# A quantised gated layer on one core: the order of the first three weight slots, and one weight turned by a transfer

## The chip, the core and the metric

The kernel runs on one core of a Trainium2 chip. The core has five engines, each with its own queue, worked off in order: TensorE (PE) multiplies matrices out of the on-chip memory SBUF into the accumulators (PSUM, eight banks of 128 x 512 fp32); VectorE (DVE), ScalarE (ACT) and GpSimd (POOL) work element by element; SyncE (SP) issues most transfers (DMA) between main memory and SBUF, or inside SBUF. Engines wait for each other by semaphores, which the framework derives from the tiles that each instruction reads and writes. The metric is the device time of one execution in microseconds (us). Of the kernel before, three executions took 729.2, 729.31 and 729.77: a median of 729.31.

## The reference

`x` is 4 x 1024 x 512 (4 sequences, b = 0 to 3), `cond` is 4 x 128, `up_w` 4096 x 512, `down_w` 512 x 2048, all fp32.

```python
scale = cond @ norm_w.T + 1.0
h = x * (scale[:, None, :] * rsqrt(mean(x * x, -1) + 1e-6))
u = h @ up_w.T
val, gate = split(u, 2, axis=-1)
h = val * gelu(gate)                       # 2048 columns
hq = round(h * 127 / max|h| per row), undone again
wq = weights of down_w as -1, 0, 1 times their mean size
out = hq @ wq.T + x
```

## The kernel before

**Tiles and batches.** A batch is one sequence, 1024 tokens, held as two halves (h = 0, 1) of 512. The 2048 columns of `val` and of `gate` are cut into 16 slots of 128 (j = 0 to 15); weight tile Wj holds the 128 `val` rows and the 128 `gate` rows of slot j (t = 0 and t = 1). fp32 operands are split into a high and a low fp16 part, and a product is high x high + high x low + low x high. The outputs of slot j are kept in SBUF in tile `H`, piece j; the pieces of `H` not yet in use (8 to 17, and 4 to 7 at the start) hold weights, tokens and scratch.

**Batch 0** multiplies plainly: `plain_half(j, h)` does 12 matmuls for the gate (`pg`), then Gelu on ScalarE, then 12 for the value (`pv`), then one VectorE instruction that joins the two. Between the two products it can call a function, `between`. `plain_first` is the same for slot 0, half 0, with its 24 matmuls in another order, and it calls `second_part` after 6 and `second_slot` after 16 of them.

**Batches 1 to 3** use a fast matrix product with seven products for eight (`slot`, `product`, lines 594 to 604 and 668 to 721). It needs sums and differences of quarters of each Wj. Those are made during batch 0: `s_sums` (POOL, into scratch `sf`), `s_high` (ScalarE), `s_low` (POOL) make seven fp16 planes, and `s_spill` writes them to main memory. `s_load_x` and `s_load_y` bring them back, for each slot of each later batch, on SP's queue.

**How a weight gets ready.** `w_load` brings the fp32 rows, `w_range` finds a power of two for each row (VectorE), `w_scale` scales them (POOL for j < `ROWS`, else ScalarE), and then the tile has to be turned, columns to rows:

- for j < `ROWS` (0, 1, 2): `w_turn` with TensorE transposes into two banks `pw`, `w_high` (ScalarE) and `w_low` (VectorE) out of them, and `w_evac` copies both banks to `wf(j)` in fp32, from which `s_sums` reads the turned quarters;
- for j >= `ROWS` (3 to 15): `w_rows` splits the rows into high (ScalarE) and low (VectorE), and one transposing transfer on SP (line 359) turns them. `s_sums` reads the unturned rows, the spilled sums are rows, and `s_load` turns them when it loads (its `turn`, line 427).

**How the tokens of batch 0 get ready.** `first_load` brings 2 x 128 tokens, `first_sum(n)` sums squares (ScalarE or VectorE), `rsqrt` makes the factors (for token groups 4 to 7: one VectorE instruction, then a power on POOL), `first_scale(n)` scales, `first_turn(n)` turns with four TensorE transposes, `first_high` and `first_low` write the fp16 parts. Groups 0 to 3 are half 0, groups 4 to 7 half 1; `other_half` turns half 1.

**Order.** The schedule is written out by hand: each engine runs its instructions in the order of the program text, and nothing is reordered. Before slot 3 the halves run in the order (0,0), (1,0), (2,0), (0,1), (1,1), (2,1); from slot 3 on `first_batch(j)` does both halves of a slot. In the later batches a small planner (`Filler`, lines 1246 to 1269) puts VectorE and ScalarE work for the previous batch into the slots by cost and due time; it is not touched. `cond_scale_rest`, `cond_largest` (VectorE), `cond_over` (a transpose on TensorE, `pm`), `cond_range` (VectorE) and `cond_spread` (TensorE, `pd`) prepare the scale of batches 1 to 3.

Lines that the prediction names: 343 transposes of weights, 358 and 359 the row split and its transfer, 367 to 379 `w_high` and `w_low`, 383 `w_evac`, 403 and 407 the sums, 615 and 658 the plain products, 935 and 937 `first_sum`, 964 `first_scale`, 985 warm-up matmuls, 289 and 286 weight loads, 924 token loads.

Of the kernel before, what the change touches and what calls it, by code (L numbers as in the profile page):

```python
# [39 lines left out]
Y_FROM, Y_TO = 3, 5  # L40
# [11 lines left out]
def glu_quant_kernel(  # L52
# [17 lines left out]
    NK = D // P  # L70
    NJ = FF // P
# [102 lines left out]
    def cond_load_rest():  # L174
        v = cond[1:].rearrange("b c -> (b c)").partition_broadcast(P)
        ACT.dma_start(out=cb[:, 1:].rearrange("p b c -> p (b c)"), in_=v)
# [90 lines left out]
    sg0 = sm.tile([P, NJ, 2], F32, name="sg_0", tag="sg")  # L267
    up_v = up_w.rearrange("(t j p) d -> j p t d", t=2, p=P)
    W_SLOT = {1: 12, 2: 13, 0: 14}
    W_EARLY = {6: 9, 7: 10, 8: 11}  # L270
    ROW_SLOT = {3: 8, 4: 15, 5: 16}
    iv = {}
    pw = {}

    def wn(j):
        return H[:, W_EARLY.get(j, W_SLOT[j % 3])]

    def wf(j):

        return H[:, 11 if j == 2 else 15 + j % 2].rearrange("p t (n f) -> p (t n) f", n=2)  # L280

    sf = H[:, 17].rearrange("p t (n f) -> p (t n) f", n=2)

    def w_load(j, ts=(1, 0)):
        if j > 2:
            SP.dma_start(out=wn(j), in_=up_v[j])
            return
        for t in ts:
            SP.dma_start(out=wn(j)[:, t], in_=up_v[j][:, t])
# [27 lines left out]
    def w_range(j, t0=0, t1=2):  # L317
        w_factor(j, w_largest(j, t0, t1), t0, t1)

    def w_gain(j):  # L320
        DVE.tensor_tensor(sg0[:, j, :], sw[:, j, :], dx[:, 0:1].to_broadcast([P, 2]), ALU.mult)

    ROWS = 3
    LATE = 6

    def w_scale(j, ts=(1, 0), eng=None):
        eng = eng or (ACT if j >= ROWS else POOL)
        for t in ts:  # L330
            w, r = wn(j)[:, t], iv[j][:, t : t + 1]
            if eng is ACT:
                ACT.activation(w, w, AF.Copy, scale=r)
            else:
                eng.tensor_scalar(w, w, r, 1.0, ALU.mult, ALU.mult)

    def w_turn(j, banks=None, ts=(1, 0)):
        if j not in pw:
            pw[j] = banks or [po_bank(f"pw_{j}_{t}") for t in (1, 0)]
        for t in ts:  # L340
            n = 1 - t
            for k in range(NK):
                PE.transpose(
                    pw[j][n][:, k * P : (k + 1) * P], wn(j)[:, t, k * P : (k + 1) * P], ident
                )
# [17 lines left out]
    def w_high(j, ts=(1, 0)):  # L363
        gate, a21, a22 = a_parts(j)
        g, v = (p.rearrange("p (n f) -> p n f", n=2) for p in pw[j])
        if 1 in ts:
            ACT.copy(gate[:, :, 0], g)
        if 0 in ts:
            ACT.copy(a21[:, 0], v[:, 0])
            ACT.copy(a22[:, 0], v[:, 1])  # L370

    def w_low(j, ts=(1, 0)):
        gate, a21, a22 = a_parts(j)
        g, v = (p.rearrange("p (n f) -> p n f", n=2) for p in pw[j])
        if 1 in ts:
            DVE.tensor_tensor(gate[:, :, 1], g, gate[:, :, 0], ALU.subtract)
        if 0 in ts:
            DVE.tensor_tensor(a21[:, 1], v[:, 0], a21[:, 0], ALU.subtract)
            DVE.tensor_tensor(a22[:, 1], v[:, 1], a22[:, 0], ALU.subtract)

    def w_evac(j):
        for n in range(2):
            ACT.copy(wf(j)[:, 2 * n : 2 * n + 2].rearrange("p n f -> p (n f)"), pw[j][n])

    def s_sums(j):
        if j >= ROWS:
            v = wn(j).rearrange("p t (n f) -> p t n f", n=2)
            a11, a12, a21, a22 = v[:, 1, 0], v[:, 1, 1], v[:, 0, 0], v[:, 0, 1]
        else:
            a11, a12, a21, a22 = (wf(j)[:, n] for n in range(4))  # L390
        POOL.tensor_tensor(sf[:, 0], a21, a22, ALU.add)
        POOL.tensor_tensor(sf[:, 2], a11, a21, ALU.subtract)
        POOL.tensor_tensor(sf[:, 1], sf[:, 0], a11, ALU.subtract)
        POOL.tensor_tensor(sf[:, 3], a12, sf[:, 1], ALU.subtract)
# [29 lines left out]
    def s_load(g, c0, c1, turn=False):  # L424
        s, d = s_tile(g)[:, c0:c1], s_dram[g % NJ, :, c0 * 2 * HALF : c1 * 2 * HALF]
        if turn:
            SP.dma_start_transpose(s.rearrange("p c w (k f) -> p (c w k) f", k=2), d)
        else:
            SP.dma_start(out=s.rearrange("p c w f -> p (c w f)"), in_=d)

    def s_load_x(g):
        s_load(g, Y_TO, C_ALL)
        s_load(g, 0, Y_FROM, g % NJ >= ROWS)

    def s_load_y(g):
        if g % NJ < ROWS:
            s_load(g, Y_FROM, Y_TO)
        else:
            s_load(g, Y_FROM + 1, Y_TO)
            s_load(g, Y_FROM, Y_FROM + 1, True)  # L440


    wmean = cpool.tile([P, 1], F32, name="wmean")
# [59 lines left out]
    def rsqrt(ssq, rs, eng=POOL):  # L503
        eng.tensor_scalar(ssq, ssq, 1.0 / D, EPS, ALU.mult, ALU.add)  # L504
        POOL.tensor_tensor(rs, ssq, neghalf[:, : rs.shape[-1]], ALU.pow)
# [129 lines left out]
    def plain_half(j, h, between=nothing):  # L635
        pg = bank(*(("A", 2) if h or j == 1 else ("B", 1)), name=f"pg_{j}_{h}")
        plain(j, 1, h, pg)
        t1 = wpool.tile([P, TOK], F32, name=f"g_{j}_{h}", tag="t1")
        ACT.activation(t1, pg, AF.Gelu, scale=gain(j, 1))
        between()  # L640
        pv = bank("E", 2, name=f"pv_{j}_{h}")
        plain(j, 0, h, pv)
        DVE.scalar_tensor_tensor(h_half(j, h), pv, gain(j, 0), t1, ALU.mult, ALU.mult)
# [279 lines left out]
    def first_load(n, m=1):  # L923
        SP.dma_start(
            out=X0[:, n : n + m],
            in_=xf[n * P : (n + m) * P, :].rearrange("(s p) d -> p s d", p=P),
        )
# [4 lines left out]
    def first_sum(n, eng=ACT):  # L932
        v, j, a = X0[:, n], junk[:, n % 4], ssq0[:, n : n + 1]
        if eng is ACT:
            ACT.activation(j, v, AF.Square, accum_out=a)
        else:
            eng.scalar_tensor_tensor(j, v, 1.0, v, ALU.mult, ALU.mult, accum_out=a)
# [21 lines left out]
    def first_scale(n, eng):  # L959
        r = rs0[:, n : n + 1]  # L960
        if eng is ACT:
            ACT.activation(X0[:, n], X0[:, n], AF.Copy, scale=r)
        else:
            eng.tensor_scalar(X0[:, n], X0[:, n], r, 1.0, ALU.mult, ALU.mult)
# [6 lines left out]
    def first_high(h, k, pt):  # L971
        c = slice(h * TOK, (h + 1) * TOK)
        ACT.activation(XP[:, 0, k, c], pt, AF.Copy, scale=scT[:, k, 0:1])

    def first_low(h, k, pt, eng=DVE):
        c = slice(h * TOK, (h + 1) * TOK)
        eng.scalar_tensor_tensor(  # L977
            XP[:, 1, k, c], pt, scT[:, k, 0:1], XP[:, 0, k, c], ALU.mult, ALU.subtract
        )

    def keep_warm(n):

        pz = bank("A", 2, name="pz")
        for i in range(n):
            PE.matmul(pz, warm[:, :P], warm, start=True, stop=True)
# [1 line left out]
    first_load(0, 2)  # L987
    first_load(2, 2)
    w_load(0)
    w_load(1)  # L990
    first_load(4, 2)
    first_load(6, 2)
    w_load(2)
    keep_warm(3)
    pc = cond_first_row()
# [4 lines left out]
    first_sum(0)  # L1000
    first_sum(1, DVE)
    root = rsqrt_root(0, 2)
    keep_warm(2)
    steps = cond_range_steps(pm, 0, 1)
    dg = next(steps)
    next(steps)
# [21 lines left out]
    w_range(0, 0, 1)  # L1028
    first_high(0, 0, ptx[0])
    w_high(0, (1,))  # L1030
    w_low(0, (1,))
    w_scale(0, (0,))
    w_gain(0)
    first_high(0, 1, ptx[1])
    first_high(0, 2, ptx[2])
    first_high(0, 3, ptx[3])
    cond_load_rest()
    w_range(1)
    w_gain(1)
# [3 lines left out]
    def second_part():  # L1043
        w_turn(0, ts=(0,))
        w_high(0, (0,))
        w_low(0, (0,))
        w_scale(1, (1,), ACT)
        for k in range(1, NK):
            first_low(0, k, ptx[k])
        ACT.activation(start_t, neghalf[:, 0:1], AF.Gelu)  # L1050


# [92 lines left out]
    def second_slot():  # L1145
        w_turn(1)
        w_high(1)
        w_low(1, (1,))
        w_range(2)
        w_gain(2)  # L1150
        w_scale(2)
        w_low(1, (0,))

    def third_slot():
        w_turn(2)
        w_high(2)
        w_low(2)
        w_evac(2)
        first_scale(4, ACT)
        first_scale(5, DVE)  # L1160
        first_scale(6, ACT)
        first_scale(7, DVE)

    def other_half():
        ptx = [po_bank(f"ptx_1_{k}") for k in range(3)] + [bank("A", 2, name="ptx_1_3")]
# [7 lines left out]
    w_load(3)  # L1173
    for n in range(4, ND):
        d_load(n)
    w_evac(0)
    w_evac(1)
    first_sum(4)
    first_sum(5)
    first_sum(6, DVE)  # L1180
    first_sum(7, DVE)
    rsqrt(ssq0[:, 4:8], rs0[:, 4:8], DVE)
    plain_half(1, 0, third_slot)
    w_load(4)
    s_sums(0)
    w_range(3)
    w_gain(3)
    plain_half(2, 0, other_half)
    w_load(5)
    for n in (2, 3):  # L1190
        d_load(n)
    w_scale(3)
    s_all(0)
    s_sums(1)
    cond_scale_rest()
    mx = cond_largest(1, B)
    plain_half(0, 1)
    w_range(4)
    w_gain(4)
    w_scale(4)  # L1200
    w_rows(3)
    s_all(1)
    s_sums(2)
    for n in D_SUM[0]:
        d_sum(n)
    pm = cond_over(mx, 1, B, "po")
    plain_half(1, 1)
    w_load(6)
    for n in (0, 1):
        d_load(n)  # L1210
# [402 lines left out]
```

## Time and profile before

The profile shows one execution; times in it are us from its first instruction.

| | us |
|---|---|
| median of three executions | 729.31 |
| the profiled execution | 728.31 |
| its span, first to last instruction | 726.5 |
| TensorE busy | 718.9 |
| VectorE busy | 582.6 |
| ScalarE busy | 398.0 |
| POOL busy | 193.4 |
| batch 0, slots 0 to 2 (TensorE's first product to slot 3) | 12.62 to 49.19 |
| batch 0, slots 3 to 15 | 49.19 to 184.69 |

A group line reads: source line, engine, operation, output <- input, shapes, count, busy us, mean ns of one, idle time before it and what ended it. In a timeline a line is: start, length, engine, line, operation, output <- input, count, and in brackets the idle time of that engine before it and its releaser. Names are those of tiles: `SXY` and part of `R` hold the turned weights, `H` weights, tokens and outputs, `pw`, `pg`, `pv`, `ptx`, `pm`, `pd`, `pz` are banks. The granted clock of TensorE is 1.00 in every slice.

### The profile page before, as it was taken

What the parts mean: (1) busy time and instruction counts of PE and PEld (TensorE: products, weight loads), DVE (VectorE), ACT (ScalarE), POOL (GpSimd) and SP (SyncE); (2) the same over time, 40 slices, a digit from 0 to 9 for tenths busy, and PEclk for the clock granted to TensorE, in tenths of its full rate; (3) what the DMA queues carried; (4) which work ended last, traced back from release to release, by engine and by line L of the source; (5) the groups of instructions that cost most, each with busy time, mean ns of one, the idle gap of its engine ahead of it and who ended that gap; (6) DMA issues with size and microseconds to landing.
All of it is one profiled execution on the core that took longest, in us unless ns stands there. A gap on an engine that the chain in (4) does not pass through costs nothing.

```text
span 726.5 us, 10149 instructions
## 1 busy us (share of the span) xinstructions
PE 718.9 (99%) x3662; PEld 359.0 (49%) x3662; DVE 582.6 (80%) x828; ACT 398.0 (55%) x627; POOL 193.4 (27%) x206
## 2 busy tenths in 40 slices
PE   8999999999999999999999999999999999999998
PEld 4544444444444446655444445665444444445844
DVE  8877888986698899788689897677678888755897
ACT  6869876772337674544335676544433665332374
POOL 1479887775100034340000030360020000000100
PEclk9999999999999999999999999999999999999999
DMA  7669999988344565867735646765934555442253
GB/s 266 223 189 298 284 291 231 252 202 231 116 102 102 131 145 139 208 161 166 179 98 103 131 102 176 201 151 163 223 102 100 84 121 103 101 102 89 97 180 115
DMA packets 203982, 117.30 MB, mean 161 GB/s; under 512 B 165382, under 2 KB 174487, under 8 KB 203932
## 3 DMA queue, kind: packets, MB, share of 16 engines
q1 hardware_dynamic: 203642, 116.33, 63.0%
q8 instruction: 28, 0.46, 0.3%
q10 hardware_dynamic: 290, 0.33, 0.2%
q14 instruction: 22, 0.18, 0.1%
HBM read 54.22 MB, written 23.09 MB: 106 GB/s over the span
## 4 chain that ended last, share of the span: by engine, by line
PE 92%; DVE 5%; DMA 1%; ACT 1%; issue 0%; SPq 0%; DVEq 0%; ACTq 0%
PE A L600 32%; PE E L600 16%; PE pg L615 11%; PE pv L615 10%; PE B L600 8%; PE po L868 8%; PE po_end L820 4%; PE po L820 1%; DVE gm L734 1%; DVE R L736 1%; DMA H<-in_x_dram 1%; DMA SXY<-H 1%; PE ptx L969 0%; PE pv L658 0%; DVE R L977 0%
## 5 line engine op out<-in xcount | busy, mean ns | idle before, releaser
L600 PEld LDWEIGHTS <-SXY 128*128 128x128 f16 x2016 | 197.2, 98 | 232.3 <-issue 0.7
L600 PE MATMUL A<-R,SXY 128*128 128x512 f16 x1152 | 266.3, 379 | 0.0
L600 PE MATMUL E<-R,SXY 128*128 128x512 f16 x576 | 140.0, 379 | 0.1
L698 DVE SCALAR_TENSOR_TENSOR H<-A,sg,t 128x512 f32<-128x512 f32 x48 | 36.0, 750 | 68.2 <-PE A L600 68.1
L792 DVE TENSOR_TENSOR H<-H,am 128x1024 f32<-128x1024 f32 x64 | 76.3, 1218 | 0.0
L615 PEld LDWEIGHTS <-SXY 128*128 128x128 f16 x486 | 47.4, 98 | 57.5 <-DMA SXY<-H 0.8
L750 POOL PARTITION_ALL_REDUCE am<-R x8 | 14.3, 1793 | 230.9 <-DVE R L736 230.9
L711 ACT ACTIVATE t<-t,sg 128x512 f32<-128x512 f32 x48 | 34.6, 721 | 69.3 <-DVE t L708 69.2
L600 PE MATMUL B<-R,SXY 128*128 128x512 f16 x288 | 70.0, 379 | 0.0
L734 DVE TENSOR_REDUCE gm<-H 128x512 f32<-128x1024 f32 x56 | 69.1, 1233 | 1.0
L615 PE MATMUL pg<-R,SXY 128*128 128x512 f16 x252 | 57.8, 379 | 0.3 <-DMA SXY<-H 0.3
L615 PE MATMUL pv<-R,SXY 128*128 128x512 f16 x234 | 54.4, 379 | 0.0
L695 ACT ACTIVATE t<-B,sg 128x512 f32<-128x512 f32 x48 | 33.0, 687 | 36.2 <-PE B L600 36.2
L678 ACT COPY t<-A 128x512 f32<-128x512 f32 x48 | 27.9, 582 | 39.8 <-PE A L600 39.5
L504 POOL TENSOR_SCALAR ssq<-ssq 128x2 f32<-128x2 f32 x12 | 3.9, 321 | 172.2 <-ACT xt L534 122.8
L868 PE MATMUL po<-wd,R 128*128 128x256 fp8e4 x384 | 48.5, 273 | 0.0
L800 ACT ACTIVATE H<-H 128x1024 f32<-128x1024 f32 x38 | 39.9, 1051 | 14.3 <-DVE H L792 14.3
L690 ACT COPY v<-E 128x512 f32<-128x512 f32 x48 | 28.1, 585 | 30.8 <-PE E L600 27.5
L868 PEld LDWEIGHTS <-R 128*128 128x128 bf16 (+1 forms) x416 | 40.7, 98 | 8.5
L717 DVE SCALAR_TENSOR_TENSOR H<-v,sg,t 128x512 f32<-128x512 f32 x48 | 38.0, 792 | 7.9 <-ACT t L711 7.9
L736 DVE TENSOR_TENSOR R<-R,gm 128x512 f32<-128x512 f32 x56 | 42.0, 750 | 1.3
L714 DVE TENSOR_TENSOR v<-A,v 128x512 f32<-128x512 f32 x48 | 32.9, 685 | 12.2 <-PE A L600 11.0
(207 smaller groups left out, 981.2 us busy)
## 6 DMA issues: line engine op xcount, KB each, us to landing
SXY<-s_dram SPq DMA_DIRECT2D x57, 256.0 KB, 3.1
s_dram<-SXY SPq DMA_DIRECT2D x18, 384.0 KB, 3.2
H<-in_L_cond_up_w_dram SPq DMA_DIRECT2D x13, 512.0 KB, 5.4
SXY<-s_dram SPq DMA_DIRECT2D x39, 128.0 KB, 3.1
xr<-in_x_dram SPq DMA_DIRECT2D x19, 256.0 KB, 3.0
out_dram<-xr SPq DMA_DIRECT2D x19, 256.0 KB, 2.5
H<-in_x_dram SPq DMA_DIRECT2D x8, 512.0 KB, 8.8
R<-in_L_cond_down_w_dram SPq DMA_DIRECT2D x8, 512.0 KB, 7.3
```

The lines of the kernel that those rows point to most:

```text
L600: PE.matmul(o, s[:, w, k, :], tv[:, :, c, l, k, :], start=start and n == 0, stop=stop and n == len(TERMS) - 1, skip_group_check=True,)
L615: PE.matmul(ps, a[k // 2][:, w, k % 2, :], XP[:, l, k, h * TOK : (h + 1) * TOK], start=n == 0, stop=n == len(terms) - 1,)
L695: ACT.activation(cur["t1"], pb, AF.Gelu, scale=gain(g, 1))
L698: DVE.scalar_tensor_tensor(h_half(g - 1, 0), prev["A"], gain(g - 1, 0), prev["t1"], ALU.mult, ALU.mult)
L711: ACT.activation(prev["t2"], prev["t2"], AF.Gelu, scale=gain(g - 1, 1))
L717: DVE.scalar_tensor_tensor(h_half(g - 1, 1), prev["v"], gain(g - 1, 0), prev["t2"], ALU.mult, ALU.mult)
L734: DVE.tensor_reduce(gm[0], v, AX.X, ALU.max, apply_absolute_value=True)
L736: return [largest, lambda: DVE.tensor_tensor(m, m, gm[0], ALU.max)]
L792: DVE.tensor_tensor(v, v, r.to_broadcast([P, 2, TOK]), ALU.mult)
L800: ACT.activation(v, v, AF.Copy, bias=MAGIC)
L820: PE.matmul(po.rearrange("p (y c o) -> p y c o", c=2, o=P), q[:, a, h, j], wd8[:, :, j // n, j % n, :, y0:y1].rearrange("p c o y -> p y c o"),
L868: PE.matmul(po, w[:, j], m, start=start and j == 0, stop=stop and j == n - 1, skip_group_check=True,)
```

## The change

- The order of the halves before slot 3 becomes (0,0), (1,0), (0,1), (1,1), (2,0), (2,1). `other_half` moves into slot 1's first half; squares and scales of token groups 4 to 7 move ahead of it, into the stretch of slot 0 and the start of slot 1.
- `ROWS` is 2: W2 goes the way of W3 to W15, over `w_rows` and a transposing transfer, and is scaled on ScalarE. `third_slot` and its TensorE transposes are gone.
- `w_evac` and `wf` are gone: the sums of W0, W1 and W2 are made of unturned rows as well, so `s_load_x` and `s_load_y` load every slot's sums with turning transfers. `s_all(0)` stands directly after W2's split, before slot 0's second half.
- Places in `H`: W3 goes to piece 11, W4 to 6 and W5 to 7 (where tokens were), in place of 14, 12 and 13, which keep the rows of W0, W1 and W2.
- W1's load stands behind the loads of token groups 4 to 7. Four warm-up matmuls stand ahead of the first `pd` in place of two.
- cond's transpose `pm` stands after slot 2's first half, in place of before slot 1's second.

```diff
--- before.py
+++ after.py
@@ -267,17 +267,13 @@
     sg0 = sm.tile([P, NJ, 2], F32, name="sg_0", tag="sg")
     up_v = up_w.rearrange("(t j p) d -> j p t d", t=2, p=P)
     W_SLOT = {1: 12, 2: 13, 0: 14}
-    W_EARLY = {6: 9, 7: 10, 8: 11}
-    ROW_SLOT = {3: 8, 4: 15, 5: 16}
+    W_EARLY = {3: 11, 4: 6, 5: 7, 6: 9, 7: 10, 8: 11}
+    ROW_SLOT = {2: 16, 3: 8, 4: 15, 5: 16}
     iv = {}
     pw = {}
 
     def wn(j):
         return H[:, W_EARLY.get(j, W_SLOT[j % 3])]
-
-    def wf(j):
-
-        return H[:, 11 if j == 2 else 15 + j % 2].rearrange("p t (n f) -> p (t n) f", n=2)
 
     sf = H[:, 17].rearrange("p t (n f) -> p (t n) f", n=2)
 
@@ -322,7 +318,7 @@
 
 
 
-    ROWS = 3
+    ROWS = 2
     LATE = 6
 
     def w_scale(j, ts=(1, 0), eng=None):
@@ -378,16 +374,9 @@
             DVE.tensor_tensor(a21[:, 1], v[:, 0], a21[:, 0], ALU.subtract)
             DVE.tensor_tensor(a22[:, 1], v[:, 1], a22[:, 0], ALU.subtract)
 
-    def w_evac(j):
-        for n in range(2):
-            ACT.copy(wf(j)[:, 2 * n : 2 * n + 2].rearrange("p n f -> p (n f)"), pw[j][n])
-
     def s_sums(j):
-        if j >= ROWS:
-            v = wn(j).rearrange("p t (n f) -> p t n f", n=2)
-            a11, a12, a21, a22 = v[:, 1, 0], v[:, 1, 1], v[:, 0, 0], v[:, 0, 1]
-        else:
-            a11, a12, a21, a22 = (wf(j)[:, n] for n in range(4))
+        v = wn(j).rearrange("p t (n f) -> p t n f", n=2)
+        a11, a12, a21, a22 = v[:, 1, 0], v[:, 1, 1], v[:, 0, 0], v[:, 0, 1]
         POOL.tensor_tensor(sf[:, 0], a21, a22, ALU.add)
         POOL.tensor_tensor(sf[:, 2], a11, a21, ALU.subtract)
         POOL.tensor_tensor(sf[:, 1], sf[:, 0], a11, ALU.subtract)
@@ -430,14 +419,11 @@
 
     def s_load_x(g):
         s_load(g, Y_TO, C_ALL)
-        s_load(g, 0, Y_FROM, g % NJ >= ROWS)
+        s_load(g, 0, Y_FROM, True)
 
     def s_load_y(g):
-        if g % NJ < ROWS:
-            s_load(g, Y_FROM, Y_TO)
-        else:
-            s_load(g, Y_FROM + 1, Y_TO)
-            s_load(g, Y_FROM, Y_FROM + 1, True)
+        s_load(g, Y_FROM + 1, Y_TO)
+        s_load(g, Y_FROM, Y_FROM + 1, True)
 
 
     wmean = cpool.tile([P, 1], F32, name="wmean")
@@ -987,9 +973,9 @@
     first_load(0, 2)
     first_load(2, 2)
     w_load(0)
-    w_load(1)
     first_load(4, 2)
     first_load(6, 2)
+    w_load(1)
     w_load(2)
     keep_warm(3)
     pc = cond_first_row()
@@ -1000,7 +986,7 @@
     first_sum(0)
     first_sum(1, DVE)
     root = rsqrt_root(0, 2)
-    keep_warm(2)
+    keep_warm(4)
     steps = cond_range_steps(pm, 0, 1)
     dg = next(steps)
     next(steps)
@@ -1028,12 +1014,14 @@
     w_range(0, 0, 1)
     first_high(0, 0, ptx[0])
     w_high(0, (1,))
+    w_scale(0, (0,))
+    first_sum(4, DVE)
     w_low(0, (1,))
-    w_scale(0, (0,))
     w_gain(0)
     first_high(0, 1, ptx[1])
     first_high(0, 2, ptx[2])
     first_high(0, 3, ptx[3])
+    first_sum(5)
     cond_load_rest()
     w_range(1)
     w_gain(1)
@@ -1044,9 +1032,13 @@
         w_turn(0, ts=(0,))
         w_high(0, (0,))
         w_low(0, (0,))
-        w_scale(1, (1,), ACT)
-        for k in range(1, NK):
-            first_low(0, k, ptx[k])
+        w_scale(1, (1,))
+        first_sum(6)
+        first_sum(7)
+        first_low(0, 1, ptx[1])
+        first_low(0, 2, ptx[2])
+        rsqrt(ssq0[:, 4:8], rs0[:, 4:8], DVE)
+        first_low(0, 3, ptx[3])
         ACT.activation(start_t, neghalf[:, 0:1], AF.Gelu)
 
 
@@ -1145,21 +1137,9 @@
     def second_slot():
         w_turn(1)
         w_high(1)
-        w_low(1, (1,))
-        w_range(2)
-        w_gain(2)
-        w_scale(2)
-        w_low(1, (0,))
-
-    def third_slot():
-        w_turn(2)
-        w_high(2)
-        w_low(2)
-        w_evac(2)
         first_scale(4, ACT)
         first_scale(5, DVE)
-        first_scale(6, ACT)
-        first_scale(7, DVE)
+        w_low(1)
 
     def other_half():
         ptx = [po_bank(f"ptx_1_{k}") for k in range(3)] + [bank("A", 2, name="ptx_1_3")]
@@ -1173,38 +1153,37 @@
     w_load(3)
     for n in range(4, ND):
         d_load(n)
-    w_evac(0)
-    w_evac(1)
-    first_sum(4)
-    first_sum(5)
-    first_sum(6, DVE)
-    first_sum(7, DVE)
-    rsqrt(ssq0[:, 4:8], rs0[:, 4:8], DVE)
-    plain_half(1, 0, third_slot)
+    first_scale(6, ACT)
+    first_scale(7, DVE)
+    w_range(2)
+    w_gain(2)
+    plain_half(1, 0, other_half)
     w_load(4)
     s_sums(0)
+    w_scale(2)
     w_range(3)
     w_gain(3)
-    plain_half(2, 0, other_half)
+    w_rows(2)
+    s_all(0)
+    s_sums(1)
+    plain_half(0, 1)
     w_load(5)
     for n in (2, 3):
         d_load(n)
     w_scale(3)
-    s_all(0)
-    s_sums(1)
     cond_scale_rest()
     mx = cond_largest(1, B)
-    plain_half(0, 1)
+    w_rows(3)
+    s_all(1)
+    s_sums(2)
+    plain_half(1, 1)
     w_range(4)
     w_gain(4)
     w_scale(4)
-    w_rows(3)
-    s_all(1)
-    s_sums(2)
     for n in D_SUM[0]:
         d_sum(n)
+    plain_half(2, 0)
     pm = cond_over(mx, 1, B, "po")
-    plain_half(1, 1)
     w_load(6)
     for n in (0, 1):
         d_load(n)
```

## The prediction

> **What bounds the kernel now.** I read the page first, then the chain of work, TensorE's waits, and the first 50 us instruction by instruction.
>
> ```profile
> span 726.5 us, 10149 instructions
> PE 718.9 (99%) x3662; PEld 359.0 (49%) x3662; DVE 582.6 (80%) x828; ACT 398.0 (55%) x627; POOL 193.4 (27%) x206
> PE 92%; DVE 5%; DMA 1%; ACT 1%; issue 0%; SPq 0%; DVEq 0%; ACTq 0%
> ```
>
> TensorE is busy for 718.9 of 726.5 us and carries 92% of the chain. So a change helps only if it takes work or idle time from TensorE, and hurts only if TensorE must wait. TensorE's waits, all of them (us in total, times, longest):
>
> ```profile
> PE pz L985 <- DVE eps L915: 1.5, 1, 1.5
> PE pg L658 <- ACT SXY L367: 0.7, 1, 0.7
> PE pd L236 <- DVE newton L953: 0.5, 1, 0.5
> PE po L868 <- DVE xr L909: 0.5, 1, 0.5
> PE pg L615 <- DMA SXY<-H: 0.3, 1, 0.3
> PE pm L211 <- DVE mx L204: 0.2, 1, 0.2
> PE pg L658 <- ACT R L973: 0.2, 1, 0.2
> PE ptx L969 <- ACT H L962: 0.2, 1, 0.2
> ```
>
> With 3.4 us after TensorE's last matmul this is all its idle time. The change touches two of these waits, W3's transfer (`SXY<-H`) and the spread of cond (`pm`). The chain in order of time (start, us, what) shows the work that goes and the late transfer; then TensorE's timeline:
>
> ```profile
> 22.44 0.87 PE pw L343 x8
> ...
> 44.75 4.39 DMA SXY<-H
> ```
>
> ```profile
> 36.98 1.03 PE L615 MATMUL pv<-R,SXY 128*128 128x512 f16 x4
> 38.24 0.27 PE L211 MATMUL pm<-ident,mx 128*3 128x128 f32 x1 [0.23 <-DVE mx L204]
> 38.34 2.75 PE L615 MATMUL pg<-R,SXY 128*128 128x512 f16 x12
> ...
> 46.11 2.75 PE L615 MATMUL pv<-R 128*128 128x512 f16 x12
> 49.19 2.76 PE L615 MATMUL pg<-R,SXY 128*128 128x512 f16 x12 [0.32 <-DMA SXY<-H]
> ```
>
> The idle numbers understate the waits. Starts in a row are 0.216 apart (12 in the chain's 2.59), while one matmul is drawn 0.379 long. By starts, the four from 36.98 hand on at 37.84 and `pm` comes at 38.24: 0.40 lost, not 0.23. The twelve from 46.11 hand on at 48.70 and slot 3 starts at 49.19: 0.49, not 0.32.
>
> **Removed from TensorE.** (1) W2's eight transposes, 0.87 us, stand in the chain and go. (2) W3's transfer is late because W3's scaling and row split stand behind cond's sums and three slots' work. Afterwards VectorE's row split of W3 ends at about 37.9 (below), its transfer lands 4.4 later, at 42.3, and slot 3 starts at 47.6: the 0.49 goes. (3) cond's maximum `mx` is ready near 36.7, and its transpose now stands after slot 2's first half, at 42.3: the 0.40 goes. Together 1.76 us, the most that this change can take away. ScalarE's six evacuations (L383, 0.59 each) go too, but ScalarE is not in the chain: nothing.
>
> **The first stage, where work is added.** Squares and scales of tokens 4 to 7 move from 22 to 27 us into the stretch from 12 to 22 us, where VectorE holds TensorE closely:
>
> ```profile
> 11.98 0.17 DVE L307 RECIPROCAL iv<-sw 128x1 f32<-128x1 f32 x1
> 12.60 0.69 DVE L376 TENSOR_TENSOR SXY<-pw,SXY 128x512 f16<-128x512 f32 x1 [0.46 <-ACT SXY L367]
> 13.21 0.15 DVE L321 TENSOR_TENSOR sg<-sw,dx 128x2 f32<-128x2 f32 x1
> 13.27 1.21 DVE L294 TENSOR_REDUCE wam<-H 128x2 f32<-128x1024 f32 x1
> ```
>
> (4) `first_sum(4)` is put before `w_low(0)`: 0.65 us (L937's step on VectorE, 7.61 to 8.26) in a gap of 0.46, so what follows on VectorE is about 0.11 late (a start of 12.71 for 12.60). Behind it stand W1's range, the first low token part and W0's low value part, on which TensorE waits: its matmul at 16.22 starts 0.09 after that part ends (15.71 + 0.42). There is no cover: +0.11 on TensorE.
>
> (5) W1's load goes behind tokens 4 to 7, two queue places. Its range can start on VectorE at 13.38. When does W1 land? L289's loads landed 6.0 to 6.5 us after issue: W1's last, issued near 3.7, by 10.2, with 2.36 MB asked for up to it. Now 3.41 MB stand up to it; at the 397 GB/s of 9 to 12 us that is 2.6 later, 12.8. The other row is the load that had that queue place before, tokens 6 and 7: issued at 5.1, landed 8.8 later, at 13.9. So VectorE waits 0 to 0.52; I take 0.4, nearer to the row of the same place. All of it goes through to TensorE, as in (4).
>
> (6) `first_sum(6)`, `(7)` stand on ScalarE before Gelu's table and `w_high(1)`, in place of one scaling (0.73): `w_high(1)` starts at 18.4 for 17.72, its gate part is done by 19.0, and TensorE asks at 19.68. Hidden. `rsqrt` on VectorE puts 0.1 before the last `first_low`, done at 18.65, wanted at 18.71. Hidden, barely. W1's second scaling goes to POOL (0.69, done at 16.7, wanted at 17.1): hidden.
>
> (7) `first_scale(5)` waits for POOL's power (1.06, from 18.05 to 19.1), and all of `w_low(1)` is queued behind it on VectorE; before, its gate part ran at 18.35. Then 0.8 and 0.65: done at 20.6, wanted at 20.64 (19.78 and four matmuls of 0.216). L964 took 0.49 with POOL idle and 0.78 and 0.95 beside POOL, which now starts W0's sums at 19.1: done between 20.3 and 20.75. 0 to 0.2, I take 0.1. [...]
>
> (8) The two further warm-up matmuls fill TensorE's 0.55 before `pd`, which waits for VectorE until 7.2. At 0.216 each they fit. At the half speed of the first (0.43) they would delay `pd` 0.4, but the transposes only start at 9.37: 0 to 0.2, taken as 0.
>
> **From 19.8 us on.** TensorE's order is then slot 1's gate, 16 transposes (1.75), value, and eight half-products of 2.59 up to slot 3. Token scales: 4 and 5 at 20, 6 at 21.3, 7 at 22.5 to 22.8, wanted from 22.4 to 23.9. Hidden. W2's split: W2's scaling on ScalarE (1.33, from 26.2), its cast (1.03) to 28.5, VectorE's low part behind W3's range, at 30.9. Its transfer lands 4.4 later (L359's median), at 35.3, and slot 2 starts at 37.1: 1.8 to spare; with L359's longest, 6.8, a stall of 0.6. I take 0.
>
> ```profile
> DMA to landing us min/median/max: 4.2/4.4/6.8
> ```
>
> W0's sums: POOL from 19.1 to 22.1, low part from 29.6 to 33, spill after W2's transfer. VectorE then does cond's sums (33.97 to 38.10 before, now 32.6 to 36.7) and W3's split, 37.9. ScalarE's Gelu of slot 1's second half stands behind W1's high sums, which wait for POOL until 34.6; it ends at 36.5 and frees a bank asked for only at 53. Slot 2's Gelu stands behind W4's scaling and two sums of down's weights (1.25 each), ends at 45.4, and its bank is asked for at 47.6. W4's load waits for the transposes of tokens 4 and 5 (23.3), W4 is read at 38.6. W4's split is transferred at 50.4 and wanted at 58.3. All hidden.
>
> **SP's queue.** W2 adds one transposing issue (1.9 at L359's shortest), at 31, with nothing urgent behind it. In the later batches slots 0, 1 and 2 load two pieces by transposing transfers (1.2 to 1.4 on SP, landing 3.7, for 0.3 to 0.9 and 3.1), 18 in all. The tightest is slot 17's load, from 184.3: landed by 190, wanted at 192.46. Slots 3 to 15 do this already, and TensorE waits nowhere there. Nothing.
>
> **Sum.** -0.87 - 0.49 - 0.40 + 0.11 + 0.4 + 0.1 = -1.15 us, all ahead of 50 us, where TensorE carries the rest on; the two stretches of VectorE in the chain (303.8 and 421.5) start from TensorE and move with it. The profiled execution took 728.31 (span 726.5), so 727.2; the median of the runs, 729.31, is 1.0 above it, so 728.15, given as 728.2. By the bounds of (4) to (8) and W2's 0.6: from -1.65 to -0.1.
>
> **Rivals.** Full gain and more: W1 and POOL's power cost nothing (-1.65), and the other executions, 1.0 us longer than the profiled one, spend some of that in W3's transfer, whose wait goes whole. For it: a wait ended by a transfer is the kind that varies (4.2 to 6.8 at L359). Against: nothing shows where the 1.0 lies. With half of it: -2.15, 727.2.
>
> W2's transfer late: for it, L359's longest; against, the transfer channels have little to do near 31 us (41 GB/s from 30 to 35). Stall 0.6: -0.55, 728.8.
>
> Slower: W1 is late by far. W3's slot is free from the start now, so W3 and down's loads leave SP from 9 us on, which before waited on SP until 14.97. If transfers under way share the channels, W1 lands with W2, W3 and two of down's loads, 5.5 MB: 3.88 MB are through by 13, and 1.6 MB at 390 GB/s make it 17.2. VectorE and TensorE wait 3.8 in place of 0.4: +2.25, 731.6. It decides (slower by 1.46) from a landing near 16.4. Against: W1 landed by 10.2 before though 1 MB of tokens was already asked for behind it. [...]
>
> **Chances.** 0.2% is 1.46 us, about what a measurement of this kernel can tell from no change. The sum 0.53, of which 0.13 with W1 in time by 13.5 passes 1.46 (faster) and 0.40 is the same; full gain and more 0.25 (faster); W2 late 0.08 (same); W1 far late 0.14 (slower). So 0.38, 0.48, 0.14. Range 727.0 to 729.8: below it lies a W3 wait longer than the profiled by more than 0.6, above it W1's case. The sum's own range is 727.7 to 729.2.
>
> **What would show it.** Eight PE transposes fewer at L343; no wait of `pg` for `SXY<-H` near 48 us; slot 3 starting near 48.1 for 49.19. Against me: VectorE idle before W1's range at 13.4 by more than 0.5, a new TensorE wait for W2's transfer `R<-H`, or a wait of a matmul from 185 us on for a transposed load.

## The result

The changed kernel takes 727.52 us in the median of 16 executions (726.76 to 728.64), the kernel before 728.83 in the median of 16 (727.62 to 730.6). The ratio is 0.9984 with a 95% interval of 0.9976 to 0.9992: faster by 0.16%, 1.2 to 1.3 us, less than the 0.2% that the prediction set as a clear difference. The forecast was 1.15 us less. The profiled execution took 727.02 us, its span is 725.2 (before 728.31 and 726.5).

All of TensorE's waits in the changed kernel (us in total, times, longest; line 644 was 658, 601 was 615, 971 was 985):

```profile
PE pz L971 <- DVE eps L901: 1.5, 1, 1.5
PE pg L644 <- ACT SXY L363: 0.7, 1, 0.7
PE pg L601 <- DMA SXY<-H: 0.4, 1, 0.4
PE pd L236 <- DVE dg L225: 0.3, 1, 0.3
PE pg L644 <- ACT R L959: 0.2, 1, 0.2
```

The wait of `pm` is gone, as forecast. The wait of slot 3 for W3's transfer, which was to go, is still there and no shorter. The chain says why (start, us, what):

```profile
40.49 0.22 PE pv L601 x2
40.71 8.02 DMA SXY<-H
48.73 0.05 issue
48.77 2.76 PE pg L601 x12
```

Before, this transfer took 4.39 us from its issue to its landing. Now it takes 8.02. It starts 4.0 us earlier and lands only 0.4 earlier; counted from slot 0's first matmul, which falls 0.65 later in this profile, it starts 4.7 earlier and lands 1.06 earlier. So slot 3 still starts when this transfer lands.

**What to compare.** The first part of an execution is not steady: the first tokens land between 5.4 and 7.0 us in the profiled executions below, and slot 0's first matmul falls between 12.6 and 15.1. So I count from slot 0's first matmul to slot 3's first, by starts, and separately what comes after.

| profiled execution | slot 0's first | slot 3's first | stretch | wait for W3's transfer (idle column) |
|---|---|---|---|---|
| before | 12.62 | 49.19 | 36.57 | 0.32 |
| before, again | 13.24 | 49.78 | 36.54 | 0.30 |
| changed | 13.27 | 48.77 | 35.50 | 0.41 |
| changed, again | 12.97 | 48.62 | 35.65 | 0.47 |
| `loads_early` | 13.20 | 48.19 | 34.99 | none |
| `both` | 12.87 | 47.68 | 34.81 | none |
| `both_again` | 13.06 | 48.54 | 35.48 | none, 0.5 for W1 |
| `w2_by_pe` | 15.08 | 51.48 | 36.40 | none |
| `w1_first` | 13.69 | 49.49 | 35.80 | 0.65 |
| `w1_behind` | 13.02 | 54.82 | 41.80 | 0.67, and 3.29 for W1 |
| `before_pm_later` | 13.16 | 49.73 | 36.57 | 0.71 |
| `before_w3_early` | 13.36 | 49.05 | 35.69 | none |

The change is worth 36.56 - 35.58 = 0.98 us in this stretch (means of two profiled executions each). After slot 3's first matmul everything is alike (batch 1 starts 135.3 later, 135.6 in `w1_first`, and TensorE's last stretch 510.1 after that), except for two waits that come and go, below.

### The profile page after: what moved, and what is told of

The parts are those of the page before. It is cut to its first block, busy times and chain, and to the rows that moved or that the text cites. A ratio compares the mean times of both kernels' runs of the same rounds, so it can differ in the third digit from the quotient of the medians.

```text
span 725.2 us, 10130 instructions
## 1 busy us (share of the span) xinstructions
PE 718.7 (99%) x3656; PEld 358.4 (49%) x3656; DVE 583.2 (80%) x824; ACT 396.4 (55%) x622; POOL 195.9 (27%) x205
## 4 chain that ended last, share of the span: by engine, by line
PE 97%; DMA 2%; ACT 0%; DVE 0%; issue 0%; SPq 0%; ACTq 0%
PE A L586 34%; PE E L586 17%; PE pg L601 11%; PE pv L601 10%; PE B L586 9%; PE po L854 8%; PE po_end L806 4%; DMA SXY<-H 1%; PE po L806 1%; DMA H<-in_x_dram 1%; PE ptx L955 1%; PE pv L644 0%; PE po_B L854 0%; PE pg L644 0%; PE pw L339 0%; PE po_E L854 0%
## 5 line engine op out<-in xcount | busy, mean ns | idle before, releaser
L676 ACT COPY v<-E 128x512 f32<-128x512 f32 x48 | 28.1, 585 | 30.9 <-PE E L586 27.7
L703 DVE SCALAR_TENSOR_TENSOR H<-v,sg,t 128x512 f32<-128x512 f32 x48 | 37.9, 790 | 7.9 <-ACT t L697 7.9
```

The source lines that it names most:

```text
L703: DVE.scalar_tensor_tensor(h_half(g - 1, 1), prev["v"], gain(g - 1, 0), prev["t2"], ALU.mult, ALU.mult)
```

## Is the rest chance? Both kernels once more

The two profiles also differ at the head (0.65 us in the changed kernel's disfavour) and near 319 us (0.5 in its favour). Nothing is edited here.

> The kernel before once more, one look. Two numbers differ between the two profiles without a reason in the change: the first tokens land at 5.50 us before and at 6.32 after (TensorE's first token transpose at 9.37 and at 10.02), and TensorE waits 0.53 us for VectorE (po from xr) near 319 us before and not at all after. Theory A (both are chance from execution to execution): the first transpose falls anywhere between 9.2 and 10.2 here, and the wait near 319 us is there or not, between 0 and 0.7. Theory B (both belong to the change): the transpose at 9.4 and a wait of 0.5 again. What belongs to the change by either theory is the stretch from the first token transpose to slot 3's first matmul: 39.82 us before, within 0.3 of it here.

> The changed kernel once more, one look. Theory A (chance): first token transpose between 9.2 and 10.2, wait of po near 318 us between 0 and 0.7. Theory B (the change): 10.0 and no wait. By either theory the stretch from the first token transpose to slot 3's first matmul is 38.75 within 0.3, with the wait for W3's transfer still in it (0.4 in the profile's idle column) and no wait before W1's range.

The kernel before started its first transpose at 9.98 this time, the changed one at 9.58: the order is turned round, so the difference at the head doesn't belong to the change. The kernel before had no wait near 319 us this time, but another one, near 162 us:

```profile
162.45 2.75 PE L615 MATMUL pv<-R,SXY 128*128 128x512 f16 x12 [0.47 <-DVE H L643]
```

In these twelve profiled executions the wait near 319 us is there twice (before, and `w1_behind`, which is the changed kernel with later loads) and the one near 162 four times (the second of before, the two kernels made from it below, and `loads_early`), and neither belongs to one kernel only. That they fell more often on the side of before (4 of its 4 profiled executions had one or the other, 2 of 8 on the changed side) may be chance or not; these runs don't settle it. Each is worth 0.4 to 0.7 us by starts, enough to make the 0.2 to 0.3 between the 0.98 of the stretch and the 1.2 to 1.3 of the medians, if they do fall more often there; that is not shown.

The times show one thing more. In `w2_by_pe` below, one stretch of 3.41 us at half clock (8.79 to 12.20) makes the mean granted clock of the execution 0.998. A mean of 0.998 or less stands in 10 of the 58 executions of the kernel before that were timed beside the runs below (729.7 to 731.6 us), and in none of 17 of the changed kernel. Over all kernels with the head of before it is 12 of 81, over those with the changed head, `w1_behind` aside, 1 of 54. Without them the three medians of before fall by 0.1 to 0.4 us. The two further warm-up matmuls of the change may be the reason; no run tests that.

## The transfer of W3: what made it slow

```diff
     plain_half(1, 0, other_half)
     w_load(4)
+    w_load(5)
+    for n in (2, 3):
+        d_load(n)
...
     plain_half(0, 1)
-    w_load(5)
-    for n in (2, 3):
-        d_load(n)
     w_scale(3)
```

> The changed kernel with W5's load and two of down's loads (1.5 MB) asked for directly behind W4's load, so that they leave SP near 24 us and not near 36, just ahead of W3's transfer. Theory 1 (W3's transfer took 8.0 us and not 4.4 because of these 1.5 MB and the spill of W0 around them): the transfer lands within 5 us of its issue, the wait of slot 3 for it goes, the stretch from the first token transpose to slot 3 falls from 38.75 to 38.2, and the time by 0.56 us against the changed kernel (some 726.9, ratio to before 0.9975). Rival (the transfer is slow by its own issue on SP, which took 4.5 us): the wait stays at 0.4 and the stretch at 38.75.

SP's queue in the changed kernel (start, us, what), and then in this run:

```profile
35.31 0.78 SPq L400 DMA_DIRECT2D s_dram<-SXY  x1
36.19 0.39 SPq L282 DMA_DIRECT2D H<-in_L_cond_up_w_dram  x1
36.63 1.87 SPq L444 DMA_DIRECT2D R<-in_L_cond_down_w_dram  x2
40.71 4.54 SPq L355 DMA_TRANSPOSE SXY<-H  x1
```

```profile
35.13 0.91 SPq L400 DMA_DIRECT2D s_dram<-SXY  x1
39.51 1.71 SPq L355 DMA_TRANSPOSE SXY<-H  x1
```

With the three loads out of the way the transfer is issued 1.2 us earlier and its issue takes 1.71 us for 4.54. What sets the time of issue is W0's spill (`s_dram<-SXY`), which SP waits for, in the changed kernel and then in this run (us in total, times, longest):

```profile
SPq L355 <- DMA s_dram<-SXY: 2.1, 1, 2.1
```

```profile
SPq L355 <- DMA s_dram<-SXY: 3.3, 1, 3.3
```

Counted from the end of SP's issue before it (38.5 and 36.0), the spill landed at 40.6 and 39.4, 5.3 and 4.3 us after its own issue. W3's transfer lands 4.28 us after its issue in this run (at 43.79, by its semaphore's records in the trace). The landings that the view matches to their issues, W3's not among them, were:

```profile
DMA to landing us min/median/max: 4.3/4.4/5.2
```

Slot 3 starts without a wait, and the stretch is 34.99, 0.59 below the mean of the changed kernel. The theory holds, the rival falls: without the loads SP's 4.54 us are gone too. The time is 727.04 (12 executions), ratio 0.9970 (0.9960 to 0.9979); the changed kernel's interval reaches to 0.9976, so the times alone can't tell the two apart, the profile does. W3's transfer took 8.02 us to land with 1.5 MB of loads just ahead of it on SP, and 4.28 without them. W0's spill, which was put ahead of the loads, landed 1.0 us later with them behind it than without (5.3 us after its issue for 4.3). In what way the loads hold the two up is not shown.

## Is the stretch the sum of its parts? Two edits to the kernel before

If W3's landing sets slot 3's start, then taking work from TensorE ahead of it gives nothing. First cond's transpose alone:

```diff
-    pm = cond_over(mx, 1, B, "po")
     plain_half(1, 1)
+    pm = cond_over(mx, 1, B, "po")
```

> The kernel before with cond's transpose pm alone moved, from ahead of slot 1's second half to behind it: one part of the change by itself, TensorE's wait for mx (0.40 by starts) should go. From slot 0's first matmul to slot 3's first it was 36.57 and 36.54 us in the two profiles of before, 35.50 and 35.65 in those of the changed kernel. Theory L (slot 3 starts when W3's transfer lands, in both kernels, so what TensorE alone saves ahead of it turns into a longer wait there): the stretch stays at 36.5 within 0.1, and the wait of slot 3 for the transfer grows from 0.3 to 0.7 in the profile's idle column. Rival (the sum of the prediction: every part is worth its own time): 36.15.

The stretch is 36.57, as before; the wait went from `pm` to slot 3:

```profile
PE pg L615 <- DMA SXY<-H: 0.7, 1, 0.7
```

The ratio is 0.9998 (0.9987 to 1.0008). So theory L holds: 0.40 us saved on TensorE were worth nothing by themselves. Then W3's split as well, ahead of W4's scaling:

```diff
     plain_half(0, 1)
+    w_rows(3)
     w_range(4)
     w_gain(4)
     w_scale(4)
-    w_rows(3)
     s_all(1)
...
-    pm = cond_over(mx, 1, B, "po")
     plain_half(1, 1)
+    pm = cond_over(mx, 1, B, "po")
```

> The kernel before with two lines moved and nothing else: W3's row split ahead of W4's range and scaling (on ScalarE and VectorE it stood behind them, until 44.7 us), and cond's transpose behind slot 1's second half, which alone gave nothing. Theory L (slot 3 starts when W3's transfer lands): the split is done near 40, the transfer issues once W0's spill is through, near 41.5, lands by 46 to 47, and both waits go: the stretch from slot 0's first matmul to slot 3's first falls from 36.55 to 35.66 (0.40 and 0.49 less), as far as the whole change brought it (35.50 and 35.65), with W2's eight transposes still in it. The time falls by 0.9 us, ratio 0.9988. Rival (W3's transfer is slow for another reason, as in the changed kernel): a wait of 0.3 to 0.7 stays and the stretch is above 36.

The transfer is issued at 42.31 (behind W0's spill, for 41.5 expected), and slot 3 follows slot 2 without a gap:

```profile
46.47 2.75 PE L615 MATMUL pv<-R 128*128 128x512 f16 x12
49.05 2.75 PE L615 MATMUL pg<-R,SXY 128*128 128x512 f16 x12
```

The stretch is 35.69, forecast 35.66: two moved lines in the kernel before bring the stretch as far as the whole change does, with W2's transposes still in it. In time it isn't shown: 0.9994 (0.9980 to 1.0008) holds both 0.9988 and no change, and this kernel's profile has the chance wait near 162 us.

## W2 turned by TensorE again

```diff
-    ROWS = 2
+    ROWS = 3
...
-    w_scale(2)
+    w_scale(2, eng=ACT)
...
-    w_rows(2)
+    w_turn(2)
+    w_high(2)
+    w_low(2)
```

> The changed kernel with W2 turned by TensorE's eight transposes again (as W0 and W1), everything else as changed. Theory (TensorE carries the chain, so its work counts in full): 0.87 us more from the first token transpose to slot 2, less what the wait for W3's transfer takes back, which then starts 0.87 later against the same landing: 38.75 to 39.1 to slot 3. Rival (the eight transposes are only worth what they are if nothing else waits; here W3's transfer decides): the stretch to slot 3 stays within 0.1 of 38.75, since 0.56 of the 0.87 go into the wait, and the rest must show as 0.3.

The profiled execution is the slowest of this kernel's ten (729.97; the others took 727.76 to 728.64). From the first token transpose (11.90) to slot 3 it took 39.58, above both theories, but the clock was at half for a part of the head (see `w1_behind` below); from slot 0's first matmul 36.40, 0.82 over the changed kernel. The transposes wait for W2's scaling, and slot 3 no longer waits:

```profile
29.55 1.26 PE L339 MATMUL pw<-ident,H 128*128 128x128 f32 x8 [0.20 <-ACT H L329]
30.65 2.75 PE L601 MATMUL pg<-R,SXY 128*128 128x512 f16 x12
```

By starts that is 29.18 to 30.65, 1.47 us for 0.87 of work; about 0.6 of it is taken back at slot 3, which leaves about the 0.82. So in this order of the halves W2's scaling comes too late for TensorE to turn W2 there, which I had not seen. In time the two can't be told apart: 0.9982 (0.9973 to 0.9991).

## W1's load: free where it is, and what it costs when it is late

```diff
     w_load(0)
+    w_load(1)
     first_load(4, 2)
     first_load(6, 2)
-    w_load(1)
     w_load(2)
```

> The changed kernel with W1's load back ahead of tokens 4 to 7. Theory: nothing waited for W1 in the changed kernel (VectorE went straight on to its range), so the stretch from slot 0's first matmul to slot 3 stays at 35.5 to 35.65 with the same wait at its end, unless VectorE now waits for tokens 4 before their sum, which is asked for 2.6 us later: then up to 0.5 more. Rival (step 5 of the prediction): 0.4 less up to slot 1's first matmul, from 7.07 us after slot 0's first to 6.7.

Slot 1's first matmul comes 7.10 us after slot 0's first (7.07 in the changed kernel), and VectorE goes on without a gap in both. The new place of W1's load cost nothing in these profiles; step (5)'s 0.4 is not there. The stretch is 35.80, 0.15 above what was expected, all of it in the wait for W3.

```diff
-    w_load(1)
     w_load(2)
+    w_load(3)
+    w_load(1)
...
     plain_first({6: second_part, 16: second_slot})
-    w_load(3)
```

> The changed kernel with W1 asked for behind W2 and W3 too (1 MB more ahead of it), to see what the prediction's slower case costs when it does happen. At 0.39 MB per us W1 lands 2.7 us later. Theory (VectorE's queue passes all lateness on to TensorE): VectorE idles for W1 ahead of its range by 1.3 to 2.7 us, and slot 1's first matmul, 7.07 us after slot 0's first in the changed kernel, comes that much later. The stretch to slot 3 grows by that less what the wait for W3's transfer takes back, at most 0.56: 36.3 to 37.7. Rival (TensorE has other work for that time): slot 1's first matmul at most 0.5 later.

VectorE waited 3.34 us for W1, more than the 1.3 to 2.7 expected, and slot 1's first matmul came 13.22 us after slot 0's first: 6.15 later than in the changed kernel, nearly twice the wait. The stretch is 41.80, where at most 37.7 was expected. TensorE's lines first:

```profile
20.07 1.04 PE L644 MATMUL pv<-R 128*128 128x512 f16 x2 [3.29 <-DVE R L374]
20.90 1.06 PE L644 MATMUL pv<-R,SXY 128*128 128x512 f16 x2
21.75 1.91 PE L339 MATMUL pw<-ident,H 128*128 128x128 f32 x8
```

Then five stretches of this run (start and end, length, busy time of TensorE's matmuls and loads, VectorE, ScalarE and POOL, then the granted clock, third from the end, the share of the transfer channels and GB/s):

```profile
15.35:18.75 3.40, 1.40 (x6) 0.31 (x4) 1.53 (x3) 3.33 (x8) 0.00 (x0) 1.00 1.04 405
18.75:22.15 3.40, 2.08 (x6) 1.06 (x7) 3.37 (x10) 0.00 (x0) 1.69 (x3) 0.50 0.44 176
22.15:25.55 3.40, 3.40 (x13) 2.01 (x12) 2.46 (x5) 1.99 (x5) 3.32 (x5) 0.50 0.00 0
18.70:18.80 0.10, 0.00 (x0) 0.00 (x0) 0.07 (x1) 0.01 (x1) 0.00 (x0) 0.72 0.93 369
25.50:25.60 0.10, 0.10 (x2) 0.01 (x1) 0.00 (x0) 0.10 (x1) 0.10 (x1) 0.65 0.00 0
```

The granted clock falls at 18.74 (0.72 in that tenth is 0.056 us at half), 2 us after TensorE's last matmul, and is back at 25.57: 6.83 us at half, 5.5 of them with work. In that time pairs of matmuls stand 0.83 apart for 0.43, and the eight transposes take 1.71 by starts for 0.88. So the price of a late W1 is the wait (3.29 shown, 3.45 by starts) and some 2.7 us of half clock on top: the one execution took 733.75 us. If the clock falls like this there too, the prediction's slower case (a wait of 3.8) was priced some 2.7 too low.

In the 3.40 us ahead of the fall TensorE is drawn busy for 1.40. How much work keeps the clock up is not shown. In `w2_by_pe`, where TensorE waited 1.8 us ahead of `pd` at the head, the clock fell as well:

```profile
5.35:8.75 3.40, 1.62 (x9) 0.58 (x7) 1.78 (x11) 1.02 (x3) 0.00 (x0) 1.00 0.99 325
8.75:12.15 3.40, 3.40 (x11) 1.53 (x12) 3.26 (x18) 2.86 (x6) 0.90 (x1) 0.51 1.05 398
```

Busy for 1.62 of 3.40 us, and then 3.41 us at half (8.79 to 12.20). That is part of why its slot 0 starts latest in the table, at 15.08; its first tokens landed latest as well, at 7.0.

## A version with both waits out

`loads_early`, and W1's gate low part ahead of the scaling of token group 5:

```diff
         first_scale(4, ACT)
-        first_scale(5, DVE)
-        w_low(1)
+        w_low(1, (1,))
+        first_scale(5, DVE)
+        w_low(1, (0,))
```

> The changed kernel with W5's load and two of down's loads moved up, as in the run loads_early (stretch 34.99 us, no wait for W3's transfer), and with W1's gate low part ahead of the scaling of token group 5 on VectorE, which is the 0.11 us that TensorE lost in slot 1's first product. Theory: slot 1's first product takes 2.59 us by starts for 2.70, the stretch from slot 0's first matmul to slot 3's first is 34.88, which is TensorE's own work in it plus the starting waits of slot 0; the time falls 0.1 below that of loads_early, some 1.9 below before, ratio near 0.9970. Rival: token group 5 is then late for its transpose, and TensorE waits up to 0.3 there instead: 35.0 to 35.2.

> The run both once more on this chip, for its time beside the kernel above: stretch 34.81 us within 0.1, and no wait for W3's transfer; 1.75 us below before in that stretch, so a ratio of 0.9976 if the waits that come and go later fall alike, with the kernel above 0.85 us over it.

Slot 1's first product now takes 2.59 us (19.93 to 22.52) for 2.70, and the stretch is 34.81, forecast 34.88. The times are 727.27 (8 executions), ratio 0.9973 (0.9963 to 0.9984), and 726.87 (6 executions), ratio 0.9963 (0.9950 to 0.9976): faster than the kernel before, and by its profile up to 0.77 us faster than the changed one, which the intervals don't yet separate. The second profile shows what the first didn't, step (5):

```profile
14.39 1.22 DVE L290 TENSOR_REDUCE wam<-H 128x2 f32<-128x1024 f32 x1 [0.52 <-DMA H<-in_L_cond_up_w_dram]
```

W1 landed 0.52 us after VectorE was ready for it, TensorE waited 0.5, and the stretch was 35.48, for 34.81 expected. So W1's place is tight: by its semaphore's records W1 landed 0.66 and 0.36 us before VectorE went on to it in the two profiled executions of the changed kernel, and 0.11 before in the first of this one.

## Why the prediction was right, point by point

The direction, the size (1.15 for 1.2 to 1.3) and the likeliest case (within 0.2%) were right, but two terms of the sum were wrong, by 0.6 and by 0.4, and nearly cancelled: that the size came out is in part luck. With the sizes measured below the sum is -0.87 + 0.12 - 0.40 + 0.01 + 0.11 = -1.03, for the 0.98 of the stretch. The mechanism was not the forecast one either. The sum lets slot 3 start when TensorE's own work is done; in fact slot 3 waited for W3's transfer in both kernels, so what the change is worth is how much earlier that transfer lands after slot 0's first matmul (1.06 and 0.89 us in the two pairs of profiles).

- **(1) W2's transposes, -0.87:** gone from the chain. Put back, they take more than their own time (1.47), since W2's scaling comes too late for them; 0.82 of that reaches slot 3.
- **(2) W3's wait, -0.49: the step that failed.** "Its transfer lands 4.4 later, at 42.3" took the median landing of such transfers. Split and issue were forecast at 37.9 and came at 39.2 (0.65 of that is the later head) and 40.71, since SP waited for W0's spill, and the landing took 8.02, behind 1.5 MB of loads that stand just ahead of it on SP (`loads_early`). By starts the wait is 0.56 and 0.64 in the two profiles, 0.49 and 0.47 before, so this term was +0.12 and not -0.49. The sign that the prediction named for it, no wait of `pg` for `SXY<-H` near 48 us, did not come. The spill and the three loads were in the text of the changed kernel; for this transfer the prediction counted neither.
- **(3) cond's transpose, -0.40:** the wait is gone. Its worth isn't its own: alone it was worth 0 (`before_pm_later`).
- **(4) `first_sum(4)`, +0.11:** it fitted the gap. W1's range starts 0.66 after slot 0's first matmul, 0.65 before: 0.01. The step was sized at 0.65 and took 0.60, so the +0.11 was 0.1 too high.
- **(5) W1's load, +0.4:** nothing in the two profiles of the changed kernel, 0.52 once in `both_again`. The bounds 0 to 0.52 were right, the value taken was too high.
- **(6), (8):** hidden, as forecast: slot 0's products run as before, starts 3.60 after slot 0's first matmul for the value's low part in both.
- **(7) `first_scale(5)` ahead of `w_low(1)`, +0.1:** 0.11, slot 1's first product takes 2.70 for 2.59. The scaling (line 964, now 950) took 0.96 beside POOL (19.69), like its row of 0.95 before, for 0.49 with POOL idle; `w_low`'s part took 0.68 beside POOL (20.57), for 0.69 with POOL idle before (18.35). In these rows the one was longer beside POOL and the other was not.
- **From 19.8 us on, and SP's queue:** W2's transfer, the token scales and the batches' turned loads made no TensorE wait in either profile of the changed kernel. W2's had little to spare: issued at 33.01 for 30.9, it landed at 37.42, 0.3 ahead of slot 2 (37.74), where 1.8 was forecast. "Nothing urgent behind it" on SP's queue was wrong: W3's transfer stood behind it, W0's spill and the three loads.

Of the rivals, "full gain and more" needed W3's wait to go, and it didn't; its guess that the ordinary executions spend more in that wait is not borne out by the two profiles of before (0.32 and 0.30). What varies there is the head and the two waits near 162 and 319 us. The slower case didn't come: W1 landed at 13.27 and 13.34, not near 16.4. That loads behind a transfer can hold it up does show, by 1.0 us, in W0's spill (5.3 for 4.3, `loads_early`); what a late W1 costs is shown by `w1_behind`, and for that the price was too low for want of the clock.

## What to carry to other kernels

Where one transfer ended the stretch, as here, TensorE's savings ahead of it were worth nothing until the transfer moved (0.40 us in `before_pm_later`, with the stretch at 36.57 as before): ask first what is late next, and test it by one part alone. A transfer's landing was not a constant: W3's took 8.02 us behind 1.5 MB of loads and 4.28 without them. So what stands in the same queue just ahead of it, in bytes, belongs into the sum, and moving loads that nobody waited for yet out of its way was the cheap gain (0.59 us of the stretch, `loads_early`). The median of 4.4 held for W3 only where nothing large was queued just ahead (4.37 and 4.39 in the kernel before, 4.28 in `loads_early`).

## What was not expected of the hardware

A TensorE wait of 3.3 us cost 6.15 us (`w1_behind`), because the clock stayed at half for 5.5 us of the work behind it; and in one execution a wait of 1.8 us was followed by 3.4 us at half (`w2_by_pe`), where in another one of 1.3 us (`before_again`) left the clock at 1.00. And W3's transposing transfer took from 4.28 us (`loads_early`) to 8.28 (`w1_behind`) to land, by what was queued ahead of it.
